# Two-layer graph attention on one core: norm of the first graph by tiles, and each engine's order read straight from a table instead of list-scheduled from it

## The chip, the cores and the metric

The kernel runs on one core of a Trainium2 chip. The metric is the device time of one execution in microseconds; lower is better. It is float32 throughout, except for bf16 masks.

## The reference

For each of 32 graphs with 512 nodes and 512 features the reference takes a layer norm and a ReLU, two graph-attention layers (four heads of 256 features, joined; then one head of 512), and adds the input.

```python
def gat_layer(x, mask, W, a_src, a_dst, bias, concat):
    xl = (x @ W).reshape(B, N, H, F)
    asrc = jnp.einsum('bnhf,hf->bnh', xl, a_src)
    adst = jnp.einsum('bnhf,hf->bnh', xl, a_dst)
    e = jax.nn.leaky_relu(asrc[:, :, None, :] + adst[:, None, :, :], NEG_SLOPE)
    e = jnp.where(mask[..., None], e, NEG_INF)
    attn = jax.nn.softmax(e, axis=1)
    out = jnp.einsum('bsdh,bshf->bdhf', attn, xl)
    ...
mask = (adj > 0) | jnp.eye(N, dtype=bool)[None]
h = jnp.maximum(_layernorm(x, axis=-1), 0.0)
h = jax.nn.elu(gat_layer(h, mask, W1, att_src1, att_dst1, b1, concat=True))
x = x + gat_layer(h, mask, W2, att_src2, att_dst2, b2, concat=False)
```

## The kernel before, in words

The kernel is written as a list of 15,064 jobs. A job is one piece of work on one engine: a product on PE (a group of matmuls), an activation on ACT, an elementwise operation on DVE, a DMA issue on SP, an accumulating DMA issue or a small operation on POOL. `Program.add` records each job with its engine, a planned cost and the jobs it depends on; nothing is issued until `prog.emit()` walks an order of all jobs. Within an engine the instructions then run in exactly that order, each waiting for what it depends on.

The jobs fall into a prologue (graphs 0 and 1 begin, weights are loaded and combined), turns, and an end. A turn finishes one graph's first layer (`gather1`), runs its second layer's projection (`project2`), starts the next graph's first projection (`project1`), and gathers an earlier graph's second layer (`gather2`). The 28 middle turns have 470 jobs each, with the same dependencies.

Most products of two matrices are done by seven products instead of eight (`sevens`), with sums of blocks on DVE (`sums`, `sums1`, `sums2`) and results read out of PSUM by ACT (copies) and DVE (additions). PSUM has eight tiles, `mm0` to `mm7`. One of the seven is split once more (`step`): short matmuls 129 wide, with a copy on ACT or an addition on DVE between them.

The attention scores go through these steps. `columns` puts a graph's source scores into a row by way of DRAM: tile `as` is stored to `das`, and a second DMA reads `das` back into `as` over all partitions. `first` makes, on ACT and DVE, the masked exponentials and their sums over tiles `l` from `as` (in the program, `l<-as,z` is a leaky ReLU). `second` builds the attention matrix `p` on DVE from `rr`, adds the mask from DRAM with an accumulating DMA issued by POOL (`p<-dm`), and takes the exponential on ACT (`p<-p,z`). `residual` loads tiles `t` of the input that are added at the end.

The first layer norm, `norm(b)`, takes the statistics of four tiles of 128 rows (`bn_stats`, `bn_aggr` on DVE), then for all four at once one addition on DVE, one power on POOL and one product on DVE. `norm_turn` scales each tile on ACT (`x<-x,stats`); for graphs 0 and 1, PE then transposes it (`mm<-identf,x`) and ACT copies the result into `ht`.

The first graph's projection (`project1_first`) needs `w1_sb` with two score columns that `scores1` works out on DVE from the weights and the rows `att_src`, `att_dst` (loaded into `p`).

What sets the order: `PLACES` has a number for each job of the prologue, of one turn and of the end; `ranks` repeats the turn's numbers for each turn. `order` is a list schedule: it keeps a clock for each engine, a model of the two DMA queues (`KIND`, `LATE`, `latency`) and takes, at each step, the ready job of lowest rank. So the ranks are priorities, and the modelled readiness decides as well.

Of the kernel before, what the change touches and what calls it, by code (L numbers as in the profile page):

```python
# [15 lines left out]
OP = mybir.AluOpType  # L16
# [4 lines left out]
EPS = 1e-5  # L21
# [23 lines left out]
class Banks(Slots):  # L45
# [17 lines left out]
PLACES = (  # L63
# [153 lines left out]
)  # L217
LATE = {
   
}  # L220

# [1488 lines left out]
```

## Time and profile before

| | |
|---|---|
| time, median of 3 runs | 2768.55 us (2767.8 to 2772.54) |
| the profiled execution | 2769.33 us, of which its span is 2767.6 us |
| PE | busy 2742.4 us (99%), 12,924 matmul records |
| weight loads on PE | busy 2371.8 us (86%) |
| DVE | busy 2558.2 us (92%) |
| ACT | busy 2229.1 us (81%) |
| POOL | busy 313.1 us (11%) |
| mean granted PE clock | 0.999 |
| DMA | 502.14 MB, mean 181 GB/s |

In the rows below, L514 is the helper that records ACT jobs, L517 the one for DVE, L520 SP's DMAs, L525 POOL's accumulating DMAs and L531 PE's products, so the tile names tell which job a row is. `x4` counts instructions; one matmul in float32 shows as two records. A time in brackets is how long the engine had been idle and what ended that.

### The profile page before, as it was taken

To read this page: it belongs to the slowest core of one execution; us is meant where nothing else is said; L and a number is where in the kernel's file an instruction comes from. 1 tells how busy PE (TensorE), PEld (TensorE's weight loads), DVE (VectorE), ACT (ScalarE), POOL (GpSimd) and SP (SyncE) were. 2 spreads that over 40 slices of the span, in tenths; PEclk is the share of its full clock that TensorE was granted. 3 is DMA by queue.
4 is the path that set the end of the run, shared out by engine and by line. 5 is a ranking of instruction groups with operands and counts; after the bars stand their busy time and mean duration, and the time that the engine had idled before them with its cause. 6 is when DMAs were issued, how large, how long until landed. Compare 5 with 4: busy or idle time off the path is not lost. (4 is left out here: it accounts for less than half of the span.)

```text
span 2767.6 us, 42320 instructions
## 1 busy us (share of the span) xinstructions
PE 2742.4 (99%) x12924; PEld 2371.8 (86%) x12924; DVE 2558.2 (92%) x6732; ACT 2229.1 (81%) x4907; POOL 313.1 (11%) x356
## 2 busy tenths in 40 slices
PE   7999999999999999999999999999999999999999
PEld 6788888888888888888888888888888888888887
DVE  8999999999999999999999999999999999999996
ACT  5978888778887788877888877888778788788883
POOL 0110111101111111111011111111111111101110
PEclk9999999999999999999999999999999999999999
DMA  8657766667666667667676766766676767767563
GB/s 232 176 157 182 203 167 184 187 176 194 182 183 179 182 176 196 178 175 195 173 201 172 182 187 178 192 186 180 180 188 175 201 167 180 195 165 208 162 171 112
DMA packets 375864, 502.14 MB, mean 181 GB/s; under 512 B 222804, under 2 KB 227668, under 8 KB 375636
## 3 DMA queue, kind: packets, MB, share of 16 engines
q1 hardware_dynamic: 329844, 332.68, 42.4%
q0 software_dynamic: 45792, 166.74, 25.1%
q8 instruction: 103, 1.69, 0.3%
q14 instruction: 125, 1.02, 0.1%
HBM read 316.41 MB, written 51.31 MB: 133 GB/s over the span
## 5 line engine op out<-in xcount | busy, mean ns | idle before, releaser
L531 PE MATMUL mm<-w_sb,hs 128*128 128x257 f32 (+3 forms) x2908 | 667.0, 367 | 5.1 <-ACT mm L514 3.3
L531 PEld LDWEIGHTS mm<-w_sb,hs 128*128 128x128 f32 x2908 | 539.7, 190 | 87.7 <-ACT mm L514 6.7
L525 POOL DMA_DIRECT2D p<-dm x314 | 273.2, 875 | 2295.0 <-DVE p L517 764.3
L531 PE MATMUL mm<-w_sb,ht 128*128 128x258 f32 x2112 | 528.6, 382 | 2.7 <-ACT mm L514 2.5
L531 PE MATMUL mm<-p,xl 128*128 128x258 f32 (+1 forms) x1984 | 495.8, 383 | 0.1
L531 PE MATMUL mm<-w_sb,h 128*128 128x257 f32 x2056 | 477.8, 379 | 0.0
L517 DVE SCALAR_TENSOR_TENSOR p<-rr,z 128x512 f32<-128x512 f32 (+1 forms) x636 | 456.0, 742 | 2.4 <-DMA rr<-drr 2.4
L531 PEld LDWEIGHTS mm<-w_sb,ht 128*128 128x128 f32 x2112 | 393.7, 190 | 63.6 <-ACT mm L514 6.4
L514 ACT ACTIVATE p<-p,z 128x512 f32<-128x512 f32 (+1 forms) x636 | 433.4, 720 | 17.7 <-DVE p L517 12.4
L531 PEld LDWEIGHTS mm<-w_sb,h 128*128 128x128 f32 x2056 | 389.0, 189 | 58.4 <-ACT xl L514 0.5
L531 PEld LDWEIGHTS mm<-p,xl 128*128 128x128 f32 x1984 | 367.2, 190 | 52.7 <-issue 6.0
L514 ACT ACTIVATE mm<-mm 128x257 f32<-128x257 f32 (+2 forms) x498 | 169.8, 347 | 269.2 <-PE mm L531 236.2
L514 ACT ACTIVATE l<-as,z 128x512 f32<-128x512 f32 x516 | 354.4, 716 | 30.8 <-DMA as<-das 30.7
L514 ACT ACTIVATE l<-l,low 128x512 f32<-128x512 f32 x516 | 370.3, 721 | 7.6 <-DVE low L517 6.7
L517 DVE CUSTOM_DVE_ANT_1 l<-l,mt 128x512 f32<-128x512 f32 x516 | 346.2, 681 | 28.4 <-ACT l L514 27.4
L514 ACT ACTIVATE xl<-mm 128x258 f32<-128x258 f32 (+2 forms) x748 | 269.3, 382 | 91.4 <-PE mm L531 89.8
L514 ACT ACTIVATE h<-mm,b_sb 128x256 f32<-128x256 f32 (+1 forms) x504 | 231.0, 480 | 77.3 <-PE mm L531 76.6
L531 PE MATMUL mm<-t,hs 128*128 128x258 f32 (+1 forms) x992 | 246.1, 380 | 0.0
L517 DVE TENSOR_TENSOR xl<-xl,mm 128x258 f32<-128x258 f32 x372 | 155.3, 419 | 57.9 <-PE mm L531 48.3
L531 PEld LDWEIGHTS mm<-t,hs 128*128 128x128 f32 x992 | 185.8, 190 | 25.5 <-DVE t L517 0.2
L531 PE MATMUL mm<-xl,p 128*128 128x258 f32 (+2 forms) x752 | 189.7, 388 | 1.0 <-ACT h L514 0.6
L517 DVE SCALAR_TENSOR_TENSOR h<-xr,h 128x512 f32<-128x512 f32 x256 | 172.2, 683 | 6.1 <-ACT xr L514 6.1
(137 smaller groups left out, 3706.2 us busy)
## 6 DMA issues: line engine op xcount, KB each, us to landing
p<-dm POOLq DMA_DIRECT2D x314, 512.0 KB, 5.0
rr<-drr SPq DMA_DIRECT2D x159, 512.0 KB
x<-in_x_dram SPq DMA_DIRECT2D x129, 256.0 KB
adj<-in_adj_dram SPq DMA_DIRECT2D x128, 256.0 KB
as<-das SPq DMA_DIRECT2D x64, 512.0 KB
t<-in_x_dram SPq DMA_DIRECT2D x124, 256.0 KB
out_dram<-t SPq DMA_DIRECT2D x124, 256.0 KB
dm<-m SPq DMA_DIRECT2D x64, 256.0 KB
```

What stands on the lines that cost most here:

```text
L514: prog.add("ACT", cost, reads, writes, lambda: nc.scalar.activation(*a, **k))
L517: prog.add("DVE", cost, reads, writes, lambda: f(*a, **k))
L525: lambda: nc.gpsimd.dma_start(to, at, accum_op=OP.add), size,
L531: f(*a, **k)
```

## The change

Two things change, one of them in all engines' orders.

First, `norm` handles graph 0 tile by tile: the addition, the power on POOL and the product are issued once per tile with one column each, so a tile's scale depends on that tile alone. The other graphs keep one step for all four. That adds nine jobs.

Second, the list schedule, its clock and its model of the DMA queues are gone. `ranks` yields the table's number (now in ten-thousandths of a microsecond), and `order` sorts the jobs of each engine by it. The table is a new one. Dependencies only decide how the five sorted lists are merged into one program; the order within an engine is the table's.

```diff
 PLACES = (
-    -21124, -21123, -21187, -21124, -19956, -19941, -19942, -21301, -19903, -19904, -18841, -19897, -6146, 6511,
...
+    -1395090, -1394813, -1395352, -1336208, -1397126, -1372226, -1386335, -1372220, -1269639, -1295127, -771710,
...
 )
-LATE = {
...
-}
...
     def ranks(self):
...
-            rank.append(PLACES[v] / 100 + turn * i)
-        return rank
+                yield PLACES[first + (j - first) % each] / 10000 + turn * ((j - first) // each + 1)
...
     def order(self):
-        jobs, rank = self.jobs, self.ranks()
...
-        while len(done) < n:
-            t, e = float("inf"), None
-            for q in self.ENGINES:
...
-            j = heappop(ready[e])[1]
-            self.start[j] = t
-            free[e] = t + jobs[j][1]
+        jobs, rank, done = self.jobs, list(self.ranks()), []
...
+        lines = {e: [] for e in self.ENGINES}
+        for j in sorted(range(len(jobs)), key=lambda j: (rank[j], j)):
+            lines[jobs[j][0]].append(j)
+        lines = [deque(q) for q in lines.values()]
+        while any(lines):
+            q = min((q for q in lines if q and not left[q[0]]), key=lambda q: rank[q[0]])
+            j = q.popleft()
             done.append(j)
...
-        every = [sk + (t,) for t in range(NT)]
-        rstd = st[:, :, S + A]
-        dve(TINY, every, every, nc.vector.tensor_scalar_add, rstd, st[:, :, S + 1], EPS)
-        prog.add(
-            "POOL", 1.0, every, every,
-            lambda: nc.gpsimd.tensor_tensor(rstd, rstd, half, op=OP.pow),
-        )
...
+        for ts in ([t] for t in range(NT)) if b == 0 else [range(NT)]:
+            every = [sk + (t,) for t in ts]
+            at = slice(ts[0], ts[-1] + 1)
+            rstd = st[:, at, S + A]
+            dve(TINY, every, every, nc.vector.tensor_scalar_add, rstd, st[:, at, S + 1], EPS)
+            prog.add(
+                "POOL", 1.0, every, every,
+                lambda r=rstd, n=len(every): nc.gpsimd.tensor_tensor(r, r, half[:, :n], op=OP.pow),
+            )
...
```

How the rows move is shown at three places. The first is the SP queue at the start of the program, where the first tiles, weights and score rows are loaded. Before:

```order
L520 DMA w1_sb_73<-in_L0_gnn_W1_dram 128x2x256
L520 DMA x2_90<-in_x_dram 128x512
L520 DMA x0_88<-in_x_dram 128x512
L520 DMA x3_91<-in_x_dram 128x512
L520 DMA x1_89<-in_x_dram 128x512
L520 DMA p0_102<-in_L0_gnn_att_src1_dram 128x512
L520 DMA w1_sb_73<-in_L0_gnn_W1_dram 128x2x256 x3
L520 DMA p0_102<-in_L0_gnn_att_dst1_dram 128x512
```

The same place now:

```order
L475 DMA w1_sb_73<-in_L0_gnn_W1_dram 128x2x256
L475 DMA x2_90<-in_x_dram 128x512
L475 DMA x0_88<-in_x_dram 128x512
L475 DMA x1_89<-in_x_dram 128x512
L475 DMA w1_sb_73<-in_L0_gnn_W1_dram 128x2x256
L475 DMA p0_102<-in_L0_gnn_att_src1_dram 128x512
L475 DMA w1_sb_73<-in_L0_gnn_W1_dram 128x2x256 x2
L475 DMA p0_102<-in_L0_gnn_att_dst1_dram 128x512
L475 DMA x3_91<-in_x_dram 128x512
```

The fourth tile of the graph, `x3`, now comes behind the first row of `att_dst`, which so moves from the tenth load to the ninth.

The second place is the SP queue in a middle turn, around the round trip of `as` through DRAM (`das`). Before:

```order
L520 DMA t3_109<-in_x_dram 128x512
L751 DMA_TRANSPOSE mt0_110<-m_105 128x8x128
L520 DMA drr0_118<-rr0_114 4x8x32
L520 DMA dm1_121<-m_105 128x1024
L520 DMA t1_107<-in_x_dram 128x512
L520 DMA das1_117<-as1_113 4x8x32
L520 DMA rr0_114<-drr0_118 128x1024
L520 DMA as1_113<-das1_117 128x1024
```

Now:

```order
L475 DMA dm1_121<-m_105 128x1024
L475 DMA t3_109<-in_x_dram 128x512
L475 DMA drr0_118<-rr0_114 4x8x32
L706 DMA_TRANSPOSE mt0_110<-m_105 128x8x128
L475 DMA das1_117<-as1_113 4x8x32
L475 DMA rr0_114<-drr0_118 128x1024
L475 DMA as1_113<-das1_117 128x1024
L475 DMA t1_107<-in_x_dram 128x512
```

The load of the residual tile `t1` moves from ahead of the round trip to behind it.

The third place is ACT late in a middle turn, where the exponentials of a matrix `p2` stand beside the copies of second-layer products out of PSUM (`xl2<-mm`). Before:

```order
L514 ACTIVATE p2_104<-p2_104,z3_128 128x512
L514 ACTIVATE xl2_80<-mm1_133 128x257
L514 ACTIVATE p2_104<-p2_104,z3_128 128x512
L514 ACTIVATE l2_101,low0_129<-l2_101,low0_129 128x512
L514 ACTIVATE l1_100,low1_130<-l1_100,low1_130 128x512
L514 ACTIVATE p2_104<-p2_104,z3_128 128x512
L514 ACTIVATE l1_100<-as0_112,z0_125 128x512
L514 ACTIVATE xl2_80<-mm6_138 128x257
```

Now:

```order
L469 ACTIVATE l0_99,low0_129<-l0_99,low0_129 128x512
L469 ACTIVATE low0_129<-low0_129 128x4
L469 ACTIVATE l2_101<-as0_112,z0_125 128x512
L469 ACTIVATE p2_104<-p2_104,z3_128 128x512 x4
L469 ACTIVATE l0_99<-as0_112,z0_125 128x512
L469 ACTIVATE xl2_80<-mm6_138 128x257
L469 ACTIVATE xl2_80<-mm7_139 128x257
L469 ACTIVATE xl2_80<-mm1_133 128x257
```

The four exponentials, spread over fifteen rows before, now stand together, and the copies come behind them.

More of the change, by code (lines that the diff above doesn't have):

```diff
@@ L2 @@
 from contextlib import ExitStack
-from heapq import heappop, heappush
 import concourse.bass as bass
@@ L63 @@
 PLACES = (
[153 rows of a table removed]
-)
-LATE = {
-}
[196 rows of a table added]
+)
 class Program:
-    CROSS, SAME = 0.15, 0.07
-    PAIRS = {("PE", "ACT"): 0.21, ("PE", "DVE"): 0.21, ("DVE", "POOL"): 0.58, ("POOL", "DVE"): 0.4}
-    AHEAD, MASK, OTHER = 3.5, (0.75, 1.84), 0.76
-    KIND = {
-        0.3: (0.39, 1.21, 0.1, 0.9),
-        0.76: (0.81, 1.62, 0.33, 0.64),
-        0.77: (0.44, 1.45, 0.2, 0.82),
-        0.9: (0, 1.72, 1.0, 0.41),
-        0.92: (0.48, 2.18, 0.24, 0.89),
-        0.94: (-0.2, 1.76, 0.21, 0.6),
-        1.09: (1.58, 1.56, 0.53, 0.59),
-        1.84: (0.48, 2.18, 0.24, 0.89),
-        2.23: (0.58, 1.62, 0.53, 0.4),
-    }
     ENGINES = "PE", "ACT", "DVE", "POOL", "SP"
@@ L286, in ranks @@
         turn = sum(job[1] for job in self.jobs[first : first + each] if job[0] == "PE")
-        rank, self.place = [], []
         for j in range(n):
             if j < first:
-                v, i = j, 0
+                yield PLACES[j] / 10000
             elif j < last:
-                v, i = first + (j - first) % each, (j - first) // each + 1
+                yield PLACES[first + (j - first) % each] / 10000 + turn * ((j - first) // each + 1)
             else:
-                v, i = first + each + j - last, (last - first) // each + 1
-            self.place.append(v)
-            rank.append(PLACES[v] / 100 + turn * i)
-        return rank
+                yield PLACES[first + each + j - last] / 10000 + turn * ((last - first) // each + 1)
     def order(self):
-        jobs, rank = self.jobs, self.ranks()
-        n = len(jobs)
-        after = [[] for _ in range(n)]
+        jobs, rank, done = self.jobs, list(self.ranks()), []
+        after, left = [[] for _ in jobs], [len(job[2]) for job in jobs]
         for j, job in enumerate(jobs):
@@ L305, in order @@
                 after[d].append(j)
-        left = [len(job[2]) for job in jobs]
-        ready_at, self.start, done = [0.0] * n, [0.0] * n, []
-        free, soon, ready = dict.fromkeys(self.ENGINES, 0.0), defaultdict(list), defaultdict(list)
-        wires, now, behind = {"SP": deque(), "POOL": deque()}, 0.0, {"SP": 0.0, "POOL": 0.0}
-        for j in range(n):
-            if not left[j]:
-                heappush(soon[jobs[j][0]], (0.0, j))
-        def release(j, at):
-            for s in after[j]:
-                ready_at[s] = max(ready_at[s], at(s))
-                left[s] -= 1
-                if not left[s]:
-                    heappush(soon[jobs[s][0]], (ready_at[s], s))
@@ L321, in step @@
-        def step(until):
-            nonlocal now
-            busy = [q for q in wires if wires[q] and wires[q][0][1] <= now]
-            speed = dict.fromkeys(wires, 1.0)
-            if len(busy) == 2:
-                speed["SP"], speed["POOL"] = self.kind(wires["SP"][0][0])[2:]
-            event, which = until, None
-            for q in wires:
-                if wires[q]:
-                    j, since, todo = wires[q][0]
-                    t = now + todo / speed[q] if q in busy else since
-                    if t < event:
-                        event, which = t, q
-            for q in busy:
-                wires[q][0][2] -= (event - now) * speed[q]
-                behind[q] -= (event - now) * speed[q]
-            now = event
-            if which in busy:
-                j = wires[which].popleft()[0]
-                release(j, lambda s: event + self.kind(j)[1] + LATE.get(self.place[j], 0) / 100)
-            return which is not None
@@ L344, in order @@
-        while len(done) < n:
-            t, e = float("inf"), None
-            for q in self.ENGINES:
-                if ready[q]:
-                    at = free[q]
-                elif soon[q]:
-                    at = max(free[q], soon[q][0][0])
-                else:
-                    continue
-                if q in wires:
-                    at = max(at, now + behind[q] - self.AHEAD)
-                if max(at, now) < t:
-                    t, e = max(at, now), q
-            if step(t):
-                continue
-            while soon[e] and soon[e][0][0] <= t:
-                k = heappop(soon[e])[1]
-                heappush(ready[e], (rank[k], k))
-            j = heappop(ready[e])[1]
-            self.start[j] = t
-            free[e] = t + jobs[j][1]
-            done.append(j)
-            if jobs[j][4] is not None:
-                wires[e].append([j, free[e] + self.kind(j)[0], jobs[j][4]])
-                behind[e] += jobs[j][4]
-            else:
-                release(j, lambda s: t + jobs[j][1] + self.latency(j, s))
+        lines = {e: [] for e in self.ENGINES}
@@ L371, in order @@
+        for j in sorted(range(len(jobs)), key=lambda j: (rank[j], j)):
[4 more added lines that the diff above has]
+            j = q.popleft()
+            done.append(j)
+            for k in after[j]:
+                left[k] -= 1
         return done
@@ L764, in norm @@
             dve(TINY, [sk + (t,)], [sk + (t,)], nc.vector.bn_aggr, st[:, t, S : S + A], st[:, t, :S])
-        every = [sk + (t,) for t in range(NT)]
-        rstd = st[:, :, S + A]
-        dve(TINY, every, every, nc.vector.tensor_scalar_add, rstd, st[:, :, S + 1], EPS)
-        prog.add(
-            "POOL", 1.0, every, every,
-            lambda: nc.gpsimd.tensor_tensor(rstd, rstd, half, op=OP.pow),
-        )
-        shift = st[:, :, S]
-        dve(
-            TINY, every, every, nc.vector.scalar_tensor_tensor,
-            shift, shift, -1.0, rstd, op0=OP.mult, op1=OP.mult,
-        )
+        for ts in ([t] for t in range(NT)) if b == 0 else [range(NT)]:
[7 more added lines that the diff above has]
+            )
+            shift = st[:, at, S]
+            dve(
+                TINY, every, every, nc.vector.scalar_tensor_tensor,
+                shift, shift, -1.0, rstd, op0=OP.mult, op1=OP.mult,
+            )
         ST[b] = sk, st
```

8 lines of the change are left out of this document (removed), and 347 rows, old and new, of the table PLACES.

## The prediction

> **What bounds the kernel now.** The page's first lines show PE as the engine to look at.
>
> ```profile
> span 2767.6 us, 42320 instructions
> PE 2742.4 (99%) x12924; PEld 2371.8 (86%) x12924; DVE 2558.2 (92%) x6732; ACT 2229.1 (81%) x4907; POOL 313.1 (11%) x356
> ```
>
> The products stay the same, so the change can only take or add PE idle time: 2767.6 - 2742.4 = 25.2 us. The table by stage says where it lies. Its columns are the length of the stage, then the busy time of PE, PEld, DVE, ACT and POOL, the granted clock, the DMA share and GB/s.
>
> ```profile
> 0.00:12.06 12.06, 0.00 (x0) 0.00 (x1) 5.88 (x22) 2.15 (x3) 1.74 (x7) 1.00 0.79 235
> 12.06:139.00 126.94, 124.45 (x518) 96.11 (x519) 115.63 (x390) 104.31 (x225) 14.76 (x15) 0.99 0.75 200
> 139.00:2600.00 2461.00, 2455.26 (x11684) 2141.95 (x11683) 2300.18 (x5983) 2019.05 (x4452) 282.64 (x319) 1.00 0.69 183
> 2600.00:2768.00 168.00, 162.67 (x726) 133.79 (x724) 136.48 (x339) 103.57 (x232) 13.93 (x16) 1.00 0.51 145
> ```
>
> Length less PE's busy time: 12.06 us before the first matmul, 2.49 in the rest of the prologue, 5.74 in the turns, 5.33 at the end. The list of waits names the releasers, first over the whole span, then (the last row) over the turns alone, in us, times, longest.
>
> ```profile
> PE mm L531 <- ACT x L514: 12.1, 1, 12.1
> PE mm L531 <- ACT mm L514: 5.8, 10, 1.2
> PE mm L531 <- ACT mm L514: 5.3, 9, 1.2
> ```
>
> So PE is the bound, and in the turns nine waits for ACT's copies out of PSUM are nearly all of the loss. The idle that a row shows is a little too small, since matmul ends are modelled. Three rows of the timeline size that:
>
> ```profile
> 850.03 1.03 PE L531 MATMUL mm<-w_sb,ht 128*128 128x258 f32 x4
> 850.90 1.03 PE L531 MATMUL mm<-p,xl 128*128 128x256 f32 x4
> 852.85 1.03 PE L531 MATMUL mm<-p,xl 128*128 128x256 f32 x4
> 854.69 2.01 PE L531 MATMUL mm<-w_sb,ht 128*128 128x258 f32 x8 [0.81 <-ACT mm L514]
> ```
>
> Four records take 0.87 us from start to start (850.90 - 850.03). The next after 852.85 was due at 853.72 and began at 854.69, 0.97 late where the row says 0.81. I multiply shown idle by 0.97 / 0.81 = 1.2.
>
> **The start.** The timeline of the first 15 us:
>
> ```profile
> 4.78 0.69 DVE L517 BATCH_NORM_STATS2 stats<-x 128x6 f32<-128x512 f32 x1 [3.20 <-DMA x<-in_x_dram]
> 7.32 0.70 DVE L517 BATCH_NORM_STATS2 stats<-x 128x6 f32<-128x512 f32 x1 [0.83 <-DMA x<-in_x_dram]
> 8.15 0.66 DVE L517 BATCH_NORM_STATS2 stats<-x 128x6 f32<-128x512 f32 x1
> 9.31 1.04 POOL L770 TENSOR_TENSOR stats<-stats,half 128x4 f32<-128x4 f32 x1 [8.00 <-DVE stats L517]
> 11.20 2.23 ACT L514 ACTIVATE x<-x,stats 128x512 f32<-128x512 f32 x3 [9.16 <-DVE stats L517]
> 12.06 2.82 PE L531 MATMUL mm<-identf,x 128*128 128x128 f32 x12 [12.06 <-ACT x L514]
> 13.21 0.43 DVE L517 SCALAR_TENSOR_TENSOR xr<-w_sb,p 128x256 f32<-128x256 f32 x1 [1.30 <-DMA p<-in_L_gnn_att_dst_dram]
> 14.67 5.92 PE L531 MATMUL mm<-w_sb,ht 128*128 128x258 f32 x24
> ```
>
> With the norm by tiles, the first tile no longer waits for the other three. From 7.32, when the last-but-one statistics began, to the first transpose at 12.06 are 4.74 us; the same path from the first tile at 4.78 has no second statistics in it (0.83 us, from 7.32 to 8.15), so the transposes begin near 4.78 + 4.74 - 0.83 = 8.7, 3.4 us earlier. The powers are now four. If each costs as much as the one of four columns (1.04), the first begins near 4.78 + (9.31 - 7.32) - 0.83 = 5.9 and the third ends near 9.1, still ahead of 10.35, where the single one ended; the fourth tile is late anyway, since its load moved back, and its transpose stands behind three products of eight records each in PE's order, as before.
>
> But the transposes are not all that is waited for. The first product also needs the score columns of `w1_sb`, and the row at 13.21 waits for `att_dst`, the tenth load. From the fourth load (7.32) to the tenth are 5.89 us, 0.98 each. Now it is the ninth: products start 0.98 earlier, if the 1.46 us from 13.21 to 14.67 stay. The four weight tiles of the second column block also move up (loads 11 to 14, the last was 16th), so the products behind keep up. I take **-1.0** (0 if the weights hold it, -3.4 if the transposes were the whole cause).
>
> **The rest of the prologue.** One place holds nearly all idle time: graph 1's last tile is transposed, copied, summed on DVE, and the seven products begin.
>
> ```profile
> 46.94 1.14 PE L531 MATMUL mm<-w_sb,ht 128*128 128x258 f32 x4 [0.53 <-ACT mm L514]
> 49.40 1.65 PE L531 MATMUL mm<-w_sb,hs 128*128 128x258 f32 x4 [1.32 <-DVE hs L517]
> 54.44 0.49 PE L531 MATMUL mm<-w_sb,hs 128*128 128x129 f32 x2 [0.46 <-DVE mm L517]
> 47.70:51.20 3.50, 2.18 (x8) 1.51 (x7) 3.50 (x14) 2.92 (x9) 0.00 (x0) 0.81 1.01 302
> 51.20:54.00 2.80, 2.77 (x12) 2.27 (x10) 1.75 (x6) 2.21 (x7) 0.00 (x0) 0.63 0.78 199
> ```
>
> The 0.53 us goes: the copy that PE waits for there (`mm1<-mm0`) reads a product that now stands four rows ahead of the waiting one in PE's order, and stood right ahead of it before. The wait for `hs` stays and grows a little: between the last transpose and the `hs` product stands one product of 0.87 us now, two before. I leave 1.6 us of 1.85. The 0.46 us goes: a product of 0.87 us now stands between the two short matmuls that wait on each other through DVE. Together -0.7.
>
> The last two rows show the clock at half speed for part of the time behind this wait: (1 - 0.81) x 3.50 + (1 - 0.63) x 2.80 = 1.7 us lost. It returns if the wait is shorter, and 1.6 us is close to the 1.85 that brought it, so I take -0.4 (between 0 and -1.7). [...] Prologue: **-1.1** (from +0.5 to -3.5).
>
> **The turns.** The nine waits have two main forms. In four, ACT waits for `as` before three leaky ReLUs, and the copy that PE needs stands behind them:
>
> ```profile
> 852.53 1.95 ACT L514 ACTIVATE l<-as,z 128x512 f32<-128x512 f32 x3 [2.27 <-DMA as<-das]
> 258.81 2.01 PE L531 MATMUL mm<-w_sb,ht 128*128 128x258 f32 x8 [0.43 <-ACT mm L514]
> 1196.15 2.01 PE L531 MATMUL mm<-w_sb,ht 128*128 128x258 f32 x8 [0.41 <-ACT mm L514]
> 1960.24 2.01 PE L531 MATMUL mm<-w_sb,ht 128*128 128x258 f32 x8 [0.36 <-ACT mm L514]
> ACT l L514 <- DMA as<-das: 30.7, 33, 2.3
> ```
>
> SP now issues that round trip ahead of the load of `t1`, so `as` lands up to 0.98 us earlier (the price of one load, above). All four waits (0.81, 0.43, 0.41, 0.36) are shorter than that: -2.01 x 1.2 = -2.4. `t1` is not needed before the second gather's outputs, later in the turn.
>
> In four others ACT waits for an accumulated `p`:
>
> ```profile
> 1000.46 1.33 ACT L514 ACTIVATE p<-p,z 128x512 f32<-128x512 f32 x2 [1.37 <-DMA p<-dm]
> 1002.01 0.49 PE L531 MATMUL mm<-w_sb,hs 128*128 128x129 f32 x2 [1.18 <-ACT mm L514]
> ACT p L514 <- DMA p<-dm: 5.2, 8, 1.4
> ```
>
> There the order keeps the two exponentials right ahead of the copy, with one product of cover on PE, so these stay where the DMA is late. What loosens is the rest: counting in one turn's order the pairs of PE products that are tied through one ACT or DVE job and have less than 1 us of other products between them, there are 14 before and 8 now. I take 6/14 off the other 3.3 us: -1.4 x 1.2 = -1.7. Turns: **-4.1** (-6.4 if all goes; above 0 by the rival below).
>
> **The end.** The chain of waits ends in the first row here, the timeline has the second:
>
> ```profile
> 2763.92 0.69 DVE t L517
> 2689.54 1.14 PE L531 MATMUL mm<-xl,p 128*128 128x258 f32 x4 [0.57 <-ACT h L514]
> ```
>
> Of the stage's 5.33 us, 2767.6 - 2763.9 = 3.7 is the last addition and store, unchanged. Three waits make up most of the other 1.6, the longest 0.57; I take the price of one off: **-0.5** (+1 to -1.5).
>
> The sum against the profiled execution: 2769.33 - 1.0 - 1.1 - 4.1 - 0.5 = 2769.33 - 6.7 = 2762.6. That execution lies 0.8 above the median of the runs, so against the median it is 2761.8. A change of 0.2%, 5.5 us, is about what a measurement of this kernel can tell from none.
>
> **Rivals.** First, only the start and the prologue move, and the turns come out even: new waits of the same sort replace the old ones, since the DMAs that were late are as full as before (0.69 share). For it speaks that DVE is 92% busy and its order is shuffled most; against it the loosened pairs. 2768.55 - 1.0 - 1.1 - 0.5 = 2766.0, within 0.2%.
>
> Second, the grouping of four exponentials on ACT late in the turn becomes a wait in every turn. Before, each exponential is followed by other ACT work, and copies out of PSUM stand between:
>
> ```profile
> 1394.02 0.71 ACT L514 ACTIVATE p<-p,z 128x512 f32<-128x512 f32 x1
> 1394.66 0.39 ACT L514 ACTIVATE xl<-mm 128x257 f32<-128x257 f32 x1
> 1396.97 0.71 ACT L514 ACTIVATE p<-p,z 128x512 f32<-128x512 f32 x1
> ```
>
> Now five copies stand behind all four, and a late accumulate holds them all. The waits for `p<-dm` seen so far last 5.2 / 8 = 0.65 us. In each of 28 turns that is +18.2, less the 2.6 of start, prologue and end: 2768.55 + 15.6 = 2784.2. It decides from 5.5 + 2.6 = 8.1 us in 28 turns, 0.29 us a turn. Against it: before, the third began at 1396.97, so its data is there some 3 us into the group, and the first two were there at 1394.02. A fixed order that repeats 28 times makes any such wait dear, whichever place it is at.
>
> **How the numbers follow.** The forecast, faster by 0.2% or more, has 0.56; its own range is 2753 to 2763. The first rival has 0.22, the second, with its like at other places of the turn, 0.22. The low end takes the outer bounds of the terms: -3.4 - 3.5 - 6.4 - 1.5 = -14.8, 2753.8; I put 2752. Upwards the range reaches into the second rival to 2781, which leaves out about one in ten there.
>
> **What would show it.** First transposes near 8.7 and first products near 13.7; no idle ahead of the second row of `ht` products in the prologue; the list of PE's waits in the turns without those for `as`, and ACT's wait for `as` below 20 us in all; ACT's wait for `p<-dm` not above 10 us. The forecast is wrong if PE's idle in the turns is above 5.74 us, above all if the same wait returns every 85 us or so; a start that gains more than 2 us would mean the weights did not bind it.

## The result and the profile after

The changed kernel takes 2814.34 us (median of four runs, 2813.02 to 2816.66) where the kernel before takes 2770.55 on the same chip: 1.0159 times as long, 95% interval 1.0141 to 1.0177. That is 44 us slower, outside the range that was given. The profiled execution took 2815.57 us, of which its span is 2813.7. A line of its page, and below it the table by stage with the same bounds as before, but for the end:

```profile
PE 2756.8 (98%) x12924; PEld 2370.9 (84%) x12924; DVE 2572.0 (91%) x6738; ACT 2240.8 (80%) x4907; POOL 321.3 (11%) x359
0.00:12.06 12.06, 2.10 (x9) 1.70 (x10) 5.53 (x24) 3.61 (x4) 2.39 (x9) 1.00 0.75 231
12.06:139.00 126.94, 122.45 (x500) 92.17 (x499) 113.76 (x381) 99.95 (x217) 13.71 (x15) 1.00 0.74 194
139.00:2600.00 2461.00, 2428.36 (x11516) 2109.89 (x11515) 2277.38 (x5896) 2000.25 (x4380) 286.72 (x314) 1.00 0.68 180
2600.00:2814.00 214.00, 203.86 (x905) 167.16 (x903) 175.36 (x440) 136.95 (x308) 18.51 (x21) 0.99 0.52 144
```

PE's idle time in the turns went from 5.74 us to 2461.00 - 2428.36 = 32.6. To split the whole difference I take the first product of the HALF block (`mm<-wx,hx`, the product of `step` with the copy between its halves) as a milestone that exists once in every turn. PE's timeline has it, before and then after, early in the third full turn and in the last:

```profile
403.97 0.39 PE L531 MATMUL mm<-wx,hx 128*128 128x129 f32 x2
2616.59 0.39 PE L531 MATMUL mm<-wx,hx 128*128 128x129 f32 x2
411.69 0.39 PE L486 MATMUL mm<-wx,hx 128*128 128x129 f32 x2
2654.80 0.39 PE L486 MATMUL mm<-wx,hx 128*128 128x129 f32 x2
```

Start, prologue and first turns cost 411.69 - 403.97 = 7.7 us more. The 26 turns between the milestones took 2212.6 before and 2243.1 now, 30.5 more. The rest, to the end of the span, went from 151.0 to 158.9, 7.9 more. (The change's order puts two products, 8 records or 1.7 us, behind the last milestone that stood ahead of it before. For the same work the turns cost some 32 us more and the end some 6.) The list of waits over the turns alone names the releasers, first PE's, then two of ACT's that the prediction spoke of:

```profile
PE mm L486 <- ACT h L469: 13.7, 19, 1.1
PE mm L486 <- ACT mm L469: 13.3, 16, 2.7
ACT p L469 <- DMA p<-dm: 61.8, 78, 3.1
ACT l L469 <- DMA as<-das: 24.5, 35, 1.4
```

Two stalls of PE return in most turns: each is longer than 0.2 us in 20 or 21 of the 26, and sums to some 19 us when it is taken from start to start. I call them K1 and K2. In one turn, on PE's and ACT's timelines (the first row and the last two are PE's):

```profile
1437.12 1.13 PE L486 MATMUL mm<-p,hs 128*128 128x256 f32 x4 [0.46 <-ACT h L469]
1428.71 2.56 ACT L469 ACTIVATE p<-p,z 128x512 f32<-128x512 f32 x4 [0.57 <-DMA p<-dm]
1436.61 0.82 ACT L469 ACTIVATE h<-mm,b_sb 128x256 f32<-128x256 f32 x2
1447.49 1.33 ACT L469 ACTIVATE p<-p,z 128x512 f32<-128x512 f32 x2 [1.21 <-DMA p<-dm]
1448.73 0.26 ACT L469 ACTIVATE mm<-mm 128x129 f32<-128x129 f32 x1
1447.18 1.03 PE L486 MATMUL mm<-p,xl 128*128 128x256 f32 x4
1449.04 0.49 PE L486 MATMUL mm<-wx,hx 128*128 128x129 f32 x2 [0.83 <-ACT mm L469]
```

K1 is PE's wait at 1437.12 for ACT's copy `h` at 1436.61. ACT is late there without waiting: from 1428.71 on it runs without a gap, and at 1428.71 it had waited for an accumulated `p`. K2 is PE's wait at 1449.04 for ACT's HALF copy at 1448.73, which stands behind two exponentials that waited 1.21 us for the next accumulate. So the data for ACT's exponentials come late, in two places of each turn. What makes them late is seen on POOL, which issues the accumulates, and on DVE, which writes what they add to. POOL at the end of a turn, before and then after:

```profile
1394.66 0.86 POOL L525 DMA_DIRECT2D p<-dm  x1 [4.16 <-PE mm L531]
1397.52 0.86 POOL L525 DMA_DIRECT2D p<-dm  x1 [1.99 <-DVE p L517]
1399.73 1.07 POOL L770 TENSOR_TENSOR stats<-stats,half 128x4 f32<-128x4 f32 x1 [1.35 <-DVE stats L517]
...
1418.41 1.48 POOL L727 TENSOR_TENSOR stats<-stats,half 128x4 f32<-128x4 f32 x1 [9.10 <-DVE low L472]
1419.85 0.90 POOL L480 DMA_DIRECT2D p<-dm  x1
1421.86 0.86 POOL L480 DMA_DIRECT2D p<-dm  x1 [1.11 <-DVE p L472]
```

Before, both accumulates went out and then came the next graph's norm (the power on `stats`). Now the power comes first. DVE's timeline has the reason, again before and after:

```profile
1395.81 1.41 DVE L517 SCALAR_TENSOR_TENSOR p<-rr,z 128x512 f32<-128x512 f32 x2
1397.14 0.69 DVE L517 BATCH_NORM_STATS2 stats<-x 128x6 f32<-128x512 f32 x1
...
1415.64 0.74 DVE L472 SCALAR_TENSOR_TENSOR p<-rr,z 128x512 f32<-128x512 f32 x1
1417.14 0.69 DVE L472 BATCH_NORM_STATS2 stats<-x 128x6 f32<-128x512 f32 x1 [0.76 <-DMA x<-in_x_dram]
1418.24 0.74 DVE L472 SCALAR_TENSOR_TENSOR p<-rr,z 128x512 f32<-128x512 f32 x1
1420.15 1.40 DVE L472 SCALAR_TENSOR_TENSOR p<-rr,z 128x512 f32<-128x512 f32 x2
```

Three of the four rows `p<-rr,z` now stand behind the statistics of the next graph's last tile, which wait for its load. Counted from the milestone, and as the median over 26 turns, the two issues moved from 53.85 and 56.71 us to 58.64 and 60.66: 4.8 and 4.0 us later. That was one theory among several; the runs had to decide.

### The profile page after: what moved, and what is told of

It is laid out like the page before. It is cut to its first block, busy times and chain, and to the rows that moved or that the text cites. A ratio compares the mean times of both kernels' runs of the same rounds, so it can differ in the third digit from the quotient of the medians.

```text
span 2813.7 us, 42292 instructions
## 1 busy us (share of the span) xinstructions
PE 2756.8 (98%) x12924; PEld 2370.9 (84%) x12924; DVE 2572.0 (91%) x6738; ACT 2240.8 (80%) x4907; POOL 321.3 (11%) x359
## 5 line engine op out<-in xcount | busy, mean ns | idle before, releaser
L469 ACT ACTIVATE p<-p,z 128x512 f32<-128x512 f32 (+1 forms) x636 | 422.8, 711 | 77.8 <-DMA p<-dm 65.5
L469 ACT ACTIVATE l<-as,z 128x512 f32<-128x512 f32 x516 | 356.5, 715 | 30.2 <-DMA as<-das 27.8
L472 DVE CUSTOM_DVE_ANT_1 l<-l,mt 128x512 f32<-128x512 f32 x516 | 343.8, 680 | 18.7 <-ACT l L469 15.3
```

Of the source, the lines that this page charges most:

```text
L469: prog.add("ACT", cost, reads, writes, lambda: nc.scalar.activation(*a, **k))
L472: prog.add("DVE", cost, reads, writes, lambda: f(*a, **k))
```

## The experiments

All ratios are to the kernel before, run on the same chip, with the 95% interval; one thousandth is 2.8 us. Where an expectation speaks of 27 middle turns, the edit moves 26, the 28 turns of the changed kernel less the first and the last. An edit to the table is shown by its number where one or a few jobs move, by the rows of the queue otherwise.

| run | ratio | interval |
|---|---|---|
| the change | 1.0159 | 1.0141 to 1.0177 |
| r1_table | 0.9999 | 0.9990 to 1.0008 |
| r2_turns | 1.0172 | 1.0157 to 1.0187 |
| r3_act | 1.0681 | 1.0665 to 1.0697 |
| r4_not_sp | 1.0261 | 1.0244 to 1.0278 |
| s1_half | 1.0215 | 1.0200 to 1.0230 |
| s2_h | 1.0180 | 1.0164 to 1.0195 |
| s3_acc | 1.0165 | 1.0143 to 1.0186 |
| s4_adj | 1.0177 | 1.0162 to 1.0193 |
| u1_issue | 1.0946 | 1.0929 to 1.0962 |
| u3_three | 1.0937 | 1.0921 to 1.0953 |
| x_after_ends | 1.0059 | 1.0042 to 1.0076 |
| v1_issue | 1.0424 | 1.0406 to 1.0441 |
| v2_three | 1.0425 | 1.0409 to 1.0440 |
| v3_reverse | 1.0724 | 1.0706 to 1.0742 |
| w1_hop | 1.0092 | 1.0075 to 1.0109 |
| w2_hop_k2 | 1.0092 | 1.0076 to 1.0108 |
| z1_loads | 1.0089 | 1.0072 to 1.0105 |
| z2_mask | 1.0042 | 1.0028 to 1.0056 |

### Which part, which engine

The first four kernels use the changed program with another table, in which the first and the last turn have places of their own:

```diff
     def ranks(self):
-        n, first, last = len(self.jobs), self.marks[1], self.marks[-2]
+        n, first, last = len(self.jobs), self.marks[2], self.marks[-3]
...
 PLACES = (
-    -1395090, -1394813, -1395352, -1336208, -1397126, -1372226, -1386335, -1372220, -1269639, -1295127, -771710,
+    -1000, 7000, -5000, 3000, 15000, 30400, 21200, -9000, 56400, 47200, 90000, 65600, 40400, 47200, 55600, 62400,
...
```

The numbers with + are the times at which the list schedule of the kernel before began each job. In r2_turns the middle turns' numbers are the change's, in r3_act those of ACT's jobs alone, in r4_not_sp those of all engines but SP.

**r1_table.** 

> The changed program (orders as a sorted table, first graph's norm by tiles), but the table holds the places that the kernel before had worked out, so every engine's queue is the one before, except the nine extra instructions of the norm. Theory T (the turn's new orders cost the 44 us): 2765 to 2772, since form and norm cost nothing in the turns. Rival F (the table's form or the norm by tiles costs something in every part, through semaphores or issue order): above 2780.

**r2_turns.** 

> As r1_table, but in the 27 middle turns all five engines have the order of the changed kernel; prologue, first turn, last turn and end keep the order before. Theory T: 27 of 28 turns at 1.5 us each, 2805 to 2815. Rival E (a good part of the 44 us comes from the prologue's half clock and the end): below 2795.

**r3_act.** 

> As r1_table, but ScalarE alone has the new order in the 27 middle turns. Both stalls that recur in a turn after the change end with ScalarE (K1: the copies h behind a copy ht; K2: the HALF copy behind the exponentials that wait for p<-dm). Theory S (ScalarE's order alone makes them): 2795 to 2815, with the waits for p<-dm of the size of the changed kernel (60 us). Rival D (the accumulate lands later because VectorE, GpSimd or SyncE issue it or its company later): under 2785, ScalarE's wait for p<-dm under 25 us.

**r4_not_sp.** 

> As r2_turns, but SyncE's queue keeps the order before; the other four engines have the new one in the 27 middle turns. Theory S and a variant of D with VectorE at fault: same as r2_turns, 2805 to 2815. Variant of D with SyncE at fault (the loads rr, adj and x now stand right behind the accumulate and share the DMA engines with it): 2770 to 2790, and p<-dm waits under 25 us.

r1_table is as fast as the kernel before: the sorted table and the norm by tiles cost nothing and bring nothing that can be measured. r2_turns has the whole loss and somewhat more: it lies in the order of the turns (two stretches at half speed, at 314.3 and 1017.4 us, are part of what is more). r3_act went far outside both forecasts. ACT's new order with the four other queues as before costs 188 us, yet not by late accumulates (15.0 us of waits for `p<-dm`): PE waits 49.2 us for `xl` and 46.3 for `h`. r4_not_sp, with one old queue among four new ones, is slower than with all five new, outside both forecasts. Yet against r2_turns, from which it differs by SP's queue alone, ACT's waits for `p<-dm` fell from 49.0 to 20.6 us, below the 25 that had been named as the sign of SP's part, and PE's for ACT's copies `mm` (K2) from 14.7 to 5.9. The new loss is a wait for `h`, 36.4 us where it was 15.3. So the run spoke for SP at K2, which its time alone hides. The five orders are fitted to each other, and the time after taking one engine's whole order across says little about that order. From here on the edits are single rows of the changed kernel.

### Four single rows

```diff
s1_half: job 125   -1461900 +1441200    s2_h:   job 17    -1351941 +1336000
s3_acc:  job 55    -1361582 +1342400    s4_adj: job 104   -1382800 +1410000
```

**s1_half.** 

> The changed kernel with one place of the table changed: in each turn ScalarE's HALF copy mm<-mm 128x129 (job 125) stands ahead of the last two exponentials of p, which wait for the accumulate p<-dm, not behind them. Theory K (the turn's loss is two recurring stalls of TensorE, K1 behind the copies h, K2 behind this HALF copy, about 20 us each over the turns): TensorE's wait for ScalarE's mm falls from 15 us to under 4, the time to 2792 to 2800. Rival M (the stall moves on: the exponentials end later, VectorE's p<-p and t<-p follow later, and TensorE waits for them): over 2808.

**s2_h.** 

> The changed kernel with one place changed: ScalarE's copy h<-mm,b_sb (job 17), for whose bank TensorE waits, stands ahead of the copy ht<-x and the copy xl<-mm, as before the change. Theory K: TensorE's wait for ScalarE's h falls from 15 us to under 4, the time to 2792 to 2800; with K1 gone TensorE comes 0.5 us earlier to K2, so K2 may grow by that and the gain shrink to 0 to 10 us (2804 to 2814), if K2 is set by the landing of p<-dm and that is not moved by TensorE. Rival M (ScalarE's later copies make the next wait): over 2808 without a longer K2.

**s3_acc.** 

> The changed kernel with one place changed: VectorE's fourth p<-rr,z (job 55), behind which the second accumulate p<-dm is issued, comes straight behind the third, ahead of a sum xl and a column z (0.47 us of VectorE). Theory D (K2 is set by when the accumulate is issued): the second issue comes 0.5 us earlier, ScalarE's wait for p<-dm falls from 62 us to about 48, the time by 0.4 to 0.5 us a turn to 2800 to 2806. Rival Q (the landing is set by what else is on the DMA engines, the two adj loads issued between the accumulates): no change, 2811 to 2817.

**s4_adj.** 

> The changed kernel with one place changed: SyncE issues the second of the two adj loads (job 104) behind das, rr's write and read back, not straight behind the first, so that one load of 256 KB and not two stands between the two accumulates. Rival Q: the second accumulate lands 0.6 to 1.4 us earlier (a 256 KB load's share of the DMA engines), ScalarE's wait for p<-dm falls below 45 us and the time to 2790 to 2804. Theory D: no change, 2811 to 2817.

None of the four helped. Against the interval of the change itself, s2_h, s3_acc and s4_adj are the same and s1_half is slower. In s1_half the wait for the HALF copy did go, and in its place PE waited, in every turn, for the copies `xl` behind it:

```profile
PE mm L486 <- ACT xl L469: 19.1, 29, 1.6
```

In s2_h PE's wait for `h` fell from 13.7 to 0.5 us, but waits whose releaser the trace does not show took 9.3 in 15 places, nearly all of them at the same product, and K2 stayed. s3_acc and s4_adj tried the two explanations of K2, the late issue and the loads beside it. Neither moved the time. But the load that s4_adj put off by some 1.5 us was still issued while the pair was under way, so its result does not exclude the loads. Theory K, that each stall is a copy standing a row too late, falls. As I read these waits, ACT was late as a whole at these places, and moving its rows among themselves only chooses which product finds it out.

### The late accumulates at the turn's end

u1_issue and u3_three moved the four rows `p<-rr,z` and their two issues far ahead, u3_three two more rows beside them, and x_after_ends took the change's middle turns out of it.

```diff
 u1_issue: jobs 302 to 305, 306, 307
-1963055, 1962910, 1962859, 1944683, 2101546, 1990800
+1898700, 1898600, 1898400, 1898500, 1926000, 1925000
 u3_three: these, and jobs 17 and 55 as in s2_h and s3_acc
 x_after_ends: as r2_turns, the other way round
```

**u1_issue.** 

> The changed kernel with six places changed, at the end of each turn: VectorE writes the four p2<-rr,z (jobs 302 to 305) straight behind the rows t of the turn's end, ahead of the next graph's BN_STATS, low and rr rows, and GpSimd issues their two accumulates ahead of its norm's pow, as before the change. In the changed kernel's trace these two issues stand at 1419.85 and 1421.86 us, behind stats and pow; counted from the same row of TensorE they stood some 5 us earlier before the change. Theory I (this late issue is the cause: the accumulate lands late, ScalarE waits for it with four exponentials in a row, has no slack left up to K1, and VectorE's next accumulate and with it K2 come late too): the wait for p<-dm at the turn's end goes, in all under 25 us instead of 62; K1 under 5 us; time 2768 to 2788. Rival L (a second, independent lateness at K2, by VectorE's row 55 and the adj loads): K1 goes but K2 stays, 2790 to 2800. Rival O (ScalarE's order itself has no slack, wherever the accumulate lands): over 2803.

**u3_three.** 

> As u1_issue, and beside it the places of s2_h (the copy h ahead of ht) and of s3_acc (VectorE's row 55 straight behind 54), neither of which helped alone. Theory I: what is left after u1_issue is small and these take part of it, 0 to 8 us below u1_issue. Rival L: 10 to 20 us below u1_issue. Rival O: within 3 us of u1_issue.

**x_after_ends.** 

> The changed kernel's order in the prologue, the first turn, the last turn and the end, with the order before in the 27 middle turns: what is left of the change when its middle turns are taken out. By the traces the start's 2.5 us are lost again to the half clock and the end has some 7 us of stalls where before had about 7: theory T gives 2763 to 2775. Rival E (prologue and end cost too): 2776 to 2790.

u1_issue was a faulty edit: the two issues came between the two accumulates of the group ahead, one of which (job 296) was then 8 us late, and PE stalled 6 to 8 us in each turn. It only shows what a late accumulate costs; u3_three is the same as u1_issue. x_after_ends lies above theory T's range, in rival E's. By the milestones it lost 4.4 us up to the third turn, 3.2 up to the last and 8.0 behind it. Waits where one order hands over to the other are part of the first two (the longest, 2.34 us, at 2530.80). The last is the last turn and the end of the change: they take 159.0 us here, 158.9 in the change and 151.0 before. Since each of r2_turns and x_after_ends has such places where orders meet, their losses do not add up to the change's.

The next three put the two issues right, and made the same move in the order before:

```diff
 v1_issue: as u1_issue, jobs 306, 307
-1926000, 1925000
+1943000, 1942000
 v2_three: these, and jobs 17 and 55
 v3_reverse: r1_table, DVE's rows in the middle turns; POOL's issues behind the power
-SCALAR_TENSOR_TENSOR p_102<-rr_114,z_128 128x512 x2
 BN_STATS stats_124<-x_91 128x6
...
 SCALAR_TENSOR_TENSOR stats_124<-stats_124 128x4
+SCALAR_TENSOR_TENSOR p_102<-rr_114,z_128 128x512
 TENSOR_TENSOR hs<-h_82,hs 128x1024
+SCALAR_TENSOR_TENSOR p_102<-rr_114,z_128 128x512 x2
```

**v1_issue.** 

> As u1_issue, with GpSimd's two issues behind both accumulates of the group ahead (in u1_issue they had come between them, and the one that was pushed back landed some 8 us late and cost 9 us in every turn). VectorE writes the four p2<-rr,z ahead of the next graph's BN_STATS, low and rr rows, and the two accumulates go out ahead of the norm's pow, some 5 us earlier than in the changed kernel. Theory I (the late issue at the turn's end is the cause of K1 and K2): wait for p<-dm under 25 us, K1 under 5 us, 2768 to 2788. Rival L (K2 has a lateness of its own): K1 goes, K2 stays, 2790 to 2800. Rival O (ScalarE's order has no slack wherever the accumulate lands): over 2803.

**v2_three.** 

> v1_issue with the places of s2_h and s3_acc beside it. Theory I: 0 to 8 us below v1_issue. Rival L: 10 to 20 us below v1_issue. Rival O: within 3 us of v1_issue.

**v3_reverse.** 

> The other way round: r1_table (the order before), with only those four rows of VectorE and the two issues of GpSimd moved back, in the 27 middle turns, behind the next graph's stats and pow, as the change had them; ScalarE's order stays as before. Theory I: the two accumulates land 4 to 5 us later than before, ScalarE's first exponential of this group comes 1.5 us earlier in the order than after the change, so it waits 1 to 5 us in each turn and the time rises by 25 us at the least, to 2790 to 2880. Rivals L and O (this issue has cover enough): under 2775.

v3_reverse says that in the order before this one move is enough for a loss, and a far greater one than the change's: 200 us, 7.7 us in each of 26 turns, more than the 2790 to 2880 that I expected. (Only its time is used.) v1_issue made K1 disappear and yet was 70 us slower than the change, where theory I had promised a gain; v2_three, with two more rows moved, is the same as v1_issue. The waits over the turns, and two stretches of the table by stage around one new stall:

```profile
PE mm L486 <- ACT xl L469: 54.9, 28, 2.2
PE mm L486 <- ACT h L469: 0.3, 1, 0.3
ACT l L469 <- DVE low L472: 70.8, 34, 2.6
...
1454.00:1457.40 3.40, 3.40 (x10) 2.83 (x11) 0.86 (x3) 3.37 (x9) 0.00 (x0) 0.64 0.76 238
1461.00:1470.00 9.00, 9.00 (x43) 7.87 (x42) 6.45 (x17) 7.89 (x17) 0.00 (x0) 1.00 0.34 65
```

The `p` rows had also passed four of DVE's rows `l`. ACT's `l<-l` needs those, waited up to 2.6 us a turn for them, and the copies `xl` behind it were late for PE, by some 2 us a turn. And such a stall cost twice in places: behind 13 of these 28 the granted clock went to half speed (0.64 in the first stretch, 10 matmul records in 3.4 us where 43 took 9.0).

So the `p` rows may pass the statistics, but not the three rows `l` ahead of the first of them:

```diff
 w1_hop: jobs 302 to 304, 306, 307
-1963055, 1962910, 1962859, 2101546, 1990800
+1944686, 1944685, 1944684, 1943000, 1942000
 w2_hop_k2: these, and jobs 55 and 104 as in s3_acc and s4_adj
```

**w1_hop.** 

> The changed kernel; at each turn's end VectorE's three later rows p2<-rr,z (jobs 304, 303, 302) follow straight behind the first (305), ahead of the next graph's last BN_STATS and what hangs on it, and the two accumulates go out ahead of the norm's pow; VectorE's rows l stay where they are (v1_issue had put the p2 rows ahead of four of them; K1 was gone there, but ScalarE's l<-l waited 2.6 us a turn for them and TensorE 2.2 us a turn behind that). The issues come about 3 us earlier than in the changed kernel. Theory I (K1 comes from these late accumulates): wait for p<-dm at the turn's end gone, K1 under 5 us, 0.6 us a turn less, 2788 to 2802. Rival J (any room that the p2 rows get is taken from another row that ScalarE waits for): over 2808, with a new wait at the turn's end.

**w2_hop_k2.** 

> w1_hop with the places of s3_acc and s4_adj beside it, both aimed at K2 (second accumulate 0.5 us earlier, one load of adj out of its way). If K1 and K2 are two separate lossses that add up: 8 to 16 us below w1_hop. If K2 is set by neither: within 3 us of w1_hop.

w1_hop is where theory I had put it: 0.67% (18.5 us) less than the change. The two issues come 1.7 and 2.6 us earlier than in the change, counted from the milestone. Waits over the turns:

```profile
PE mm L486 <- ACT h L469: 0.9, 1, 0.9
PE mm L486 <- ACT mm L469: 15.3, 18, 1.8
ACT p L469 <- DMA p<-dm: 43.1, 55, 2.2
```

K1 is gone (0.9 us instead of 13.7), though no row of ACT was moved; K2 is whole. And w2_hop_k2 shows that issuing K2's accumulate a little earlier (0.3 us by the trace), with one load of 256 KB moved by some 2 us, does nothing to it that the time shows.

### K2: the accumulate shares the DMA engines

The view of the DMAs gives the time from issue to landing of the two accumulates around K2, in one turn before and one after:

```profile
p<-dm POOLq DMA_DIRECT2D x2, 512.0 KB, 6.1
p<-dm POOLq DMA_DIRECT2D x2, 512.0 KB, 7.4
```

In 12.5 us around each pair the queue of the accumulates took 37.5% of the DMA engines' time before and 35.0% after, that of SP's loads 47.1 and 47.7%. Worked out from the packets of POOL's queue, as medians over 26 turns, the bytes of these two took 2.5 and 3.6 us before, 4.0 and 4.1 now. The trace has the same loads around them in both kernels, but the 512 KB of `rr` were read back some 7 us after the first issue before, and some 3 us after it now. The second issue is also later than before, counted from the milestone: at 78.45 us in the change and 77.99 in w1_hop, where it was at 76.63. z1_loads moved three loads on SP behind the read back of `as`; z2_mask also moved the row of DVE that uses one of them.

```diff
 z1_loads: SP, middle turns
 adj<-in_adj_dram
-adj<-in_adj_dram
 das<-as
-rr<-drr
-x<-in_x_dram
 as<-das
+adj<-in_adj_dram
+rr<-drr
+x<-in_x_dram
 z2_mask: DVE, middle turns
-m<-adj
 hs<-ht,hs
...
 mm<-mm,f
+m<-adj
```

**z1_loads.** 

> w1_hop with three loads of SyncE's queue moved in the 27 middle turns: the second adj (job 104), the read back of rr (353, 512 KB) and the load x (403) stand behind the read back of as (78), not ahead of it, so that they are issued some 4 to 6 us later, when the second accumulate before K2 has mostly landed. In the changed kernel these loads stand in the 3.5 us around the two accumulates, whose 512 KB took about 4 us each by the packets of the trace, against 2.5 and 3.6 us before the change. Theory Q (K2 is set by what shares the DMA engines with that accumulate): its transfer falls to about 3 us, it lands 1 us earlier or more, K2 falls from 19 us to under 6, the time from 2794 to 2772 to 2784. Rival D (K2 is set by the late issue alone): within 4 us of w1_hop. Rival J (the loads moved are then late for VectorE's m<-adj or p<-rr,z): K2 goes and a wait of VectorE or ScalarE takes its place, over 2790.

**z2_mask.** 

> z1_loads, with one row of VectorE moved back in the 27 middle turns: m<-adj (job 105), which in z1_loads waited up to 2.3 us for the load of adj that had been moved (20.5 us in all) and held up the sum mm<-mm,f behind it, for which TensorE then waited 16.4 us, now stands behind that sum. Theory Q and J together (K2 was the shared transfer; what z1_loads won was given back at this one row): TensorE's stall at this place goes, 2772 to 2782, and the table is then within 0.3 to 0.6 % of the kernel before. Rival J2 (the next row that hangs on one of the three loads, p<-rr,z or the next adj loads on SyncE's queue, makes the next wait): within 4 us of z1_loads, with that row's wait in its place.

In z1_loads the second accumulate's bytes took 2.5 us (the first's still 3.8), the wait for `p<-dm` fell by half and K2 was gone, yet the time stayed. Here are the waits over the turns, then one turn on DVE's and PE's timelines:

```profile
ACT p L538 <- DMA p<-dm: 22.9, 33, 1.2
PE mm L555 <- ACT mm L538: 1.4, 2, 0.8
DVE m L541 <- DMA adj<-in_adj_dram: 20.5, 23, 2.3
PE mm L555 <- DVE mm L541: 12.7, 21, 2.0
...
1008.38 0.43 DVE L541 TENSOR_SCALAR m<-adj 128x512 bf16<-128x512 int32 x1 [2.29 <-DMA adj<-in_adj_dram]
1010.26 0.29 DVE L541 TENSOR_TENSOR mm<-mm,f 128x129 f32<-128x129 f32 x1
1010.61 0.49 PE L555 MATMUL mm<-w_sb,hs 128*128 128x129 f32 x2 [2.00 <-DVE mm L541]
```

DVE waited for the load that had been moved, and PE for the sum behind it. z2_mask took that one row away, and the time fell to 1.0042, as expected. Its turns as the table by stage has them, and its longest waits of PE in them:

```profile
139.00:2600.00 2461.00, 2455.17 (x11663) 2139.58 (x11662) 2307.08 (x5977) 2023.20 (x4445) 284.49 (x319) 1.00 0.69 182
PE mm L555 <- issue: 1.4, 1, 1.4
PE mm L555 <- ACT mm L538: 1.3, 2, 0.6
```

PE's idle time in the turns is 5.8 us, as before the change. From the milestone in the third turn to that in the last z2_mask takes 2212.3 us, where before took 2212.6 and the change 2243.1. So the loss of the turns has two causes, both in the order around accumulates: DVE's and POOL's at the turn's end (K1), SP's loads beside a later pair (K2). For K2, moving the loads is enough: the second issue is still 0.8 us later than before in z2_mask (77.43), and yet its data land at 83.2 us from the milestone, where they landed at 83.7 before and at 86.0 in w1_hop. Whether the earlier issue alone would have been enough was tried for 0.3 us only. The 0.42% that is left is 11.7 us between the medians. By the milestones of the profiled executions 4.0 us of it lie ahead of the third turn and 7.4 behind the last milestone (1.7 of them the two products that moved there). No version of these beats the kernel before.

## Why the prediction was wrong

**The start** came out at the forecast time, in part by luck, and gained nothing. Transposes began at 9.51 us (forecast 8.7) and products at 13.72 (forecast 13.7). But the sum said that products wait for the score columns, which would come 0.98 us earlier with `att_dst`. The first row here shows that row of DVE only 0.37 us earlier (12.84, 13.21 before), and the first product waited for ACT's copy `ht`, not for DVE. And PE's clock ate the gain. Below the row of DVE stand PE's start on the timeline of the change, then two stretches of equal length from the first product, after and before:

```profile
12.84 0.43 DVE L472 SCALAR_TENSOR_TENSOR xr<-w_sb,p 128x256 f32<-128x256 f32 x1 [0.97 <-DMA p<-in_L_gnn_att_dst_dram]
9.51 1.12 PE L486 MATMUL mm<-identf,x 128*128 128x128 f32 x4 [9.51 <-ACT x L469]
11.08 1.97 PE L486 MATMUL mm<-identf,x 128*128 128x128 f32 x8 [0.45 <-ACT x L469]
13.72 6.45 PE L486 MATMUL mm<-w_sb,ht 128*128 128x258 f32 x16 [0.68 <-ACT ht L469]
...
13.70:19.10 5.40, 5.38 (x13) 4.29 (x14) 5.30 (x29) 1.29 (x2) 0.66 (x1) 1.00 1.06 367
14.60:20.00 5.40, 5.40 (x25) 4.66 (x24) 4.00 (x22) 1.47 (x4) 0.00 (x0) 1.00 1.06 384
```

In 5.4 us there were 13 matmul records instead of 25: half speed. From start to start the records of the products took 0.43 us each up to 19.2 us and 0.22 behind that; before, 0.22 from 15.8 us on. (The column says 1.00 in both, since the trace's first reading of the clock, at full speed, comes only at 19.25 us, and at 15.75 before.) This step counted time until the first product as gained, without asking at which clock it runs. By the first HALF product of the prologue the change is 0.1 us ahead (50.70, 50.84 before).

**The prologue** (-1.1) did not come. The 0.53 us ahead of the `ht` product went, the wait for `hs` stayed (1.26), the 0.46 went, and the stretch at half speed that before has from 49.88 to 53.30 us is not in the change's trace. The waits of 0.53 and 1.32 us that were held to have brought it are 1.26 us now, and the clock stays at 1.00 (46 to 55 us). The -0.4 rested on the author's estimate that 1.6 us is close to 1.85; at which length of wait the clock falls, no run shows. But from 51.5 to 55.4 us PE now waits four times, 0.42, 0.35, 0.17 and 0.35 us, and two more waits of 0.7 and 0.5 us follow up to 139 us. From the first HALF product to the next milestone the change lost 2.4 us, and 5.5 in the three turns that follow, together the 7.7. r1_table shows that the norm by tiles is not the cause; which rows of the prologue's order are was not tried.

**The turns** (-4.1) are the step that failed, with 30.5 us the other way. The step priced the waits that the trace of before showed, and took for granted that where the profile shows no wait there is cover. "These stay where the DMA is late" was said of the exponentials of K2, which were late for PE in four turns before and are in most now: SP's loads, which the change moved beside that accumulate, were not read. Nor was the order of DVE and POOL at the turn's end, which put off the other accumulate, behind K1, by 4 to 5 us. The count of pairs with little cover (14 to 8) pointed the wrong way, because cover between two rows says nothing once the engine between them arrives late. Of the `as` waits the direction was right: ACT's wait fell from 30.2 to 24.5 us, not below the 20 that was named.

**The end** (-0.5) was wrong too. From the last milestone to the end of the span the change takes 7.9 us more, 1.7 of them the products that moved there. PE's waits in it sum to 4.9 us where they were 1.2, and from PE's last product to the end, the part that the sum took as unchanged, 4.7 us pass where 3.7 did.

**The second rival** had the mechanism of K1 and too small a price: a group of four exponentials held up by a late accumulate, turn after turn. The group it pointed at did not wait; the next group of four did (1428.71), and PE felt it 8 us later at K1. K2 is of its like, at two exponentials, but stays when K1 is gone (w1_hop). It was priced at 0.65 us a turn, the mean wait before; ACT's waits for `p<-dm` became 61.8 us, some 2.2 a turn, and PE lost 30.5 / 26 = 1.2 us a turn. The sign that was named in advance, the same wait every 85 us or so and PE's idle in the turns above 5.74 us, is what the profile shows.

## What to carry to other kernels

When an order is replaced, follow each asynchronous transfer first: where its issue stands now, what its issuing engine must finish ahead of it, and what else is on the DMA engines while it moves. A stall that returns once a turn is rarely cured at the row where it shows: moving the waiting copies brought nothing, while moving the producer's rows took 18.5 us with no row of the waiting engine changed. And change a few rows at a time, since whole orders of engines are fitted to each other, and each row that is given room takes it from another one that must be named beforehand.

## What the runs showed of the hardware

An accumulate was slower with other transfers beside it: the same 512 KB took 2.5 us in z1_loads, where three of SP's loads had been moved back, and 4.1 in the change.

The clock at the start differed from run to run. In 14 profiled executions with the change's prologue the first reading of full speed lay between 12.3 and 19.3 us, though PE's first matmul varied by 0.8 us only, and the first HALF product of the prologue lay between 47.2 and 50.7 us (50.6 to 51.6 in five with the prologue before). The half-speed stretch of the kernel before, from 49.88 to 53.30 us with a granted clock of 0.50, lasted 3.41 us. v1_issue had 14 of that length, and its mean granted clock was 0.991; at half of 3.41 us each they cost, by estimate, 14 x 1.7 = 24 us of its 70. Of the 14, 13 stood behind a stall of some 2.1 us. The length of the stall alone did not decide it there: the 16 records behind one of 2.05 us (1453.96) took 5.43 us, those behind one of 2.04 us (1101.36) took 3.74.
